# Rows of factors through DRAM instead of a selecting matmul, in one attention layer and one mixture of experts

## The chip, the cores and the metric

The kernel runs on one core of a Trainium2 chip. The time is that of the device, in microseconds (us), from the first to the last instruction of one launch. A core has five engines that run side by side, each through its own list of instructions in a fixed order: TensorE (PE, matmuls; its weight loads are shown as PEld), VectorE (DVE), ScalarE (ACT), GpSimd (POOL) and SyncE (SP). SyncE computes nothing; it issues DMAs, which sixteen DMA engines carry out. SBUF is the on-chip memory of 128 partitions, PSUM the memory that matmuls write, DRAM the memory off the core.

## The reference, cut to what matters

The program is a stack of eight layers on x of 4 x 512 x 128 float32: four times an attention and a feed-forward part, each followed by a layer norm of input plus output. The change touches the last two. The attention (index 3, "third" when counted from 0) has 16 heads of 64 and learned relative positions up to 16; the feed-forward part after it is a mixture of 16 experts of width 64, of which each token uses 4, and a shared one of width 128.

```python
attn = softmax(sim)                        # 16 heads, 512 x 512 each
out = attn @ v + (attn at the offsets) @ rel_v_table
out = out.reshape(B, T, 1024) @ Wo.T + bo
...
weights = top-4 of sigmoid(x @ w_gate.T), divided by their sum + 1e-6
combine[t, e] = the weight of expert e for token t, else 0
g = silu(x @ w1_e[e].T);  u = x @ w3_e[e].T
routed[t] = sum over e of combine[t, e] * (g * u) @ w2_e[e].T
```

Two factors matter here. Softmax's division is done late: the kernel adds up exp in passing and multiplies the attention's output by 1/sum, one factor for each head and query. And combine is one factor for each expert and token.

## The kernel before

Tokens stand in four blocks b of 512 (T). At build time a planner lays out each engine's list: an instruction's priority is its place in the program, and it may be passed by others as long as the planner believes its inputs not to be ready. On the chip that order is fixed; an engine whose next instruction waits does nothing else. The Python code is made of generators: `k.step(gs)` advances each of them by one `yield`, so the number of steps between two parts of the code sets how far apart they stand in priority. `k.bank("b")` takes one of two PSUM banks that all side work shares; `k.turn` makes side work take turns for them.

**The attention, class A3.** One unit t is one pair of heads of one block: 8 pairs, 4 blocks, 32 units. A unit has 8 items: four query blocks qc of 128, two heads e. `prep` computes the pair's Q and K with three matmuls each, splits them into a high and a low part (H by ScalarE at L1307, L by VectorE at L1308) and puts them into place with twelve copies from SBUF to SBUF (L1312), ten on SyncE's queue and two on GpSimd's. It also has SyncE store relative-position scores into DRAM (L1294) and read them back shifted (W, L1297). `score` makes two matmuls into one PSUM bank (L1344, L1345), adds W (L1347), takes the extreme of each row (L1349) and has ScalarE write p = exp (L1350), with the row's sum into `den`. The tile p holds both heads of a query block and has three buffers. `turn` runs two items later: four transposes (L219), a copy to PT (L1363), and, after the second head, a store of p's diagonal band to DRAM by SyncE (L1372, tile a3dpw). After the last item the band of the whole unit is read back along the diagonals (L1376), for which SyncE waits until the stores have landed. `tail` multiplies PT by V (L1393), adds the relative part (L1406, L1407) and copies the result to OT: 128 partitions are two heads of 64, the free axis is 512 queries.

Since one factor must reach the 64 partitions of its head, `fin` works on half a block, four pairs: 1/sum (L1422), its split into two parts (L1423, L1424), four transposes into 16 rows, a copy to lT (L1430), and for each pair a matmul of lT with a table of ones, `sel` (L1436), that puts each head's row, high plus low, on 64 partitions of a PSUM bank. VectorE multiplies OT by that bank (L1437). Then 16 matmuls project OT (L1447); after the second half a layer norm ends the block. `fin` runs at units 5, 9, 13, ..., 29 and once more at the end; from the same units on `half` projects the next half's values, through the same banks.

**The experts, class F3.** One step i is two experts (or the shared one) of a block, 9 steps to a block. `hidden` makes six matmuls, silu and a product (L2279), into h: 128 partitions are two experts of 64. `weigh`, four steps later, selects the two experts' rows with a matmul of `cT` with ones (L2287) and multiplies h by them (L2288). `out` adds h times w2 into the block's result (L2297). `gate` computes the weights: scores, two rankings (with a product by GpSimd at L1924), the weights (L2253), their split (L2256, L2257), transposes, and the copy to cT (L2265). It is started `ahead` = 7 steps before its block and advances `steps` = 2 times each step.

The two tables of ones are loaded by GpSimd's queue, which also clears the tiles for the rows (`rows16`).

## Time and profile before

| | us |
|---|---|
| three runs | 2252.24, 2237.65, 2249.25 |
| median | 2249.25 |
| the profiled execution, whole time | 2239.62 |
| its span in the profile | 2237.9 |
| units 9 to 12 of the attention (1700.6 to 1770.8) | 70.2 |
| of these TensorE / VectorE / ScalarE busy | 65.1 / 56.5 / 50.8 |
| last hidden products to the end (2216.9 to 2238.0) | 21.1 |

The granted TensorE clock was 0.965 of full speed over the span. The profile comes from one execution; all times in it count from the span's start. A "group" row gives an instruction's line in the kernel, its engine, operation, written and read tiles, count, busy time and the mean of one; by shapes it gives the least, median and longest time of one. The timeline gives start, length, engine and line; SPq means that SyncE was issuing a DMA, not that the DMA was running. The chain follows the execution back from its last instruction, at each step to what released it. Matmuls are pipelined: a matmul that follows another shows up with its full length in a group, but with the distance to the next one in the chain.

### The profile page before, as it was taken

The numbers are of one execution on the slowest core, as the hardware profiler recorded it, in microseconds if no ns is written. First come the engines' busy times: TensorE is split into PE (matmuls) and PEld (weight loads), VectorE is DVE, ScalarE is ACT, GpSimd is POOL, SyncE is SP. The second block draws the span as 40 slices with busy tenths as digits, with TensorE's granted clock in tenths as the row PEclk, the third lists the DMA queues.
The fourth block names the chain that finished last, engine by engine and source line by source line (L and its number), as shares of the span: only waits on it lengthen the run. The fifth ranks groups of instructions, "written<-read, shape, count | busy, mean of one in ns | idle before, by whom it ended". The sixth has DMA issues, their size and how long they took to land.

```text
span 2237.9 us, 43122 instructions
## 1 busy us (share of the span) xinstructions
PE 2025.4 (91%) x14400; PEld 1477.7 (66%) x14400; DVE 1664.1 (74%) x5592; ACT 1333.5 (60%) x2983; POOL 501.9 (22%) x706
## 2 busy tenths in 40 slices
PE   7999788888888999999999999998999999999897
PEld 4666566676665667676887665786666566666676
DVE  5778689888878677873777785544777877778787
ACT  3566787787734656665333666333777777767632
POOL 3222212111212532433000322531111111111220
PEclk9999999999978999999999999999999999999999
DMA  5321322021433454421021420604888878888400
GB/s 171 106 77 35 109 50 57 6 48 27 116 113 108 130 175 125 127 65 57 15 67 48 116 78 15 219 17 112 214 209 198 211 192 193 199 194 211 99 5 15
DMA packets 264918, 242.10 MB, mean 108 GB/s; under 512 B 106352, under 2 KB 190618, under 8 KB 263866
## 3 DMA queue, kind: packets, MB, share of 16 engines
q1 hardware_dynamic: 259146, 221.33, 37.2%
q0 software_dynamic: 5232, 17.50, 3.3%
q8 instruction: 115, 1.88, 0.3%
q14 instruction: 105, 0.86, 0.1%
q10 hardware_dynamic: 320, 0.52, 0.1%
HBM read 103.82 MB, written 74.32 MB: 80 GB/s over the span
## 4 chain that ended last, share of the span: by engine, by line
PE 59%; DVE 17%; ACT 10%; DMA 7%; issue 4%; POOL 2%; SPq 1%; ACTq 0%; POOLq 0%; DVEq 0%
PE t L219 5%; PE s L2129 4%; PE o L1393 3%; PE o L744 3%; PE s L695 3%; PE t L728 3%; PE o L1032 3%; PE b L313 3%; PE b L219 3%; PE o L2025 3%; DMA a3dpw<-p 2%; PE s L313 2%; PE b L315 2%; PE b L314 2%; PE s L315 2%
## 5 line engine op out<-in xcount | busy, mean ns | idle before, releaser
L985 DVE CUSTOM_DVE_ANT_0 junk<-w,a1mask 128x640 bf16<-128x640 f32 x256 | 203.1, 818 | 67.3 <-PE w L983 65.4
L219 PE MATMUL t<-ident,p 128*128 128x128 f32 x1280 | 201.9, 279 | 23.8 <-ACT p L1350 15.7
L772 ACT ACTIVATE Pt<-t 128x384 f32<-128x384 f32 (+1 forms) x384 | 179.5, 528 | 65.8 <-PE t L728 54.4
L219 PEld LDWEIGHTS t<-ident,p 128*128 128x128 f32 x1280 | 151.7, 142 | 81.0 <-ACT p L1350 39.0
L1363 ACT COPY PT<-t 128x512 f32<-128x512 f32 x256 | 149.9, 596 | 71.9 <-PE t L219 70.9
L1059 ACT ACTIVATE Pt<-t 128x512 f32<-128x512 f32 x256 | 149.1, 597 | 72.7 <-PE t L1058 44.5
L1350 ACT ACTIVATE p<-s,nb 128x512 f32<-128x512 f32 x256 | 178.6, 702 | 12.8 <-DVE nb L1349 8.4
L1349 DVE TENSOR_REDUCE nb<-s 128x1 f32<-128x512 f32 x256 | 175.0, 687 | 2.6
L1368 DVE CUSTOM_DVE_ANT_0 jk<-p,a3right 128x496 bf16<-128x496 f32 (+3 forms) x256 | 125.0, 488 | 29.2 <-ACT p L1350 17.8
L697 DVE CUSTOM_DVE_ANT_0 junk<-s,a0mask 128x128 bf16<-128x128 f32 (+3 forms) x256 | 114.2, 485 | 43.4 <-PE s L695 42.4
L697 DVE CUSTOM_DVE_ANT_0 junk<-s,a2mask 128x128 bf16<-128x128 f32 (+3 forms) x256 | 114.9, 484 | 28.3 <-PE s L695 27.9
L781 POOL TENSOR_SCALAR_AFFINE_SELECT Pt<-Pt 128x512 f32<-128x512 f32 x112 | 69.9, 636 | 249.0 <-ACT Pt L772 248.9
L1344 PE MATMUL s<-a3KT,a3QT 128*128 128x512 f32 x256 | 118.9, 465 | 7.3 <-DMA a3K<-L 4.1
L1347 DVE TENSOR_TENSOR s<-s,W 128x160 f32<-128x160 f32 (+1 forms) x256 | 81.1, 318 | 56.1 <-PE s L1345 55.2
L1393 PE MATMUL o<-PT,V 128*64 128x512 f32 x512 | 116.9, 599 | 0.5 <-ACT PT L1363 0.5
L1707 ACT ACTIVATE p<-sm,nb 128x128 f32<-128x128 f32 x256 | 100.6, 396 | 24.8 <-DVE nb L1705 24.3
L1345 PE MATMUL s<-a3K,a3Q 128*128 128x512 f32 x256 | 102.7, 401 | 0.1
L1705 DVE CUSTOM_DVE_ANT_0 sm<-s,band,rn 128x128 f32<-128x128 f32 x256 | 78.3, 344 | 26.5 <-PE s L1692 19.3
L1056 PE MATMUL t<-a1Q,a1K 128*128 128x512 f32 (+3 forms) x256 | 92.4, 366 | 6.2 <-ACT Pt L1059 3.6
L695 PE MATMUL s<-a0K,a0Q 128*128 128x256 f32 (+2 forms) x256 | 83.6, 387 | 14.0 <-DVE mx L697 6.8
L982 PE MATMUL w<-a1K,a1Q 128*128 128x256 f32 (+2 forms) x192 | 83.8, 437 | 9.3 <-DVE mx L985 8.3
L2012 ACT ACTIVATE sl<-s 128x512 f32<-128x512 f32 x64 | 38.0, 598 | 91.0 <-PE s L315 85.6
(494 smaller groups left out, 5812.7 us busy)
## 6 DMA issues: line engine op xcount, KB each, us to landing
W<-a3dsk SPq DMA_DIRECT2D x32, 640.0 KB
a1Q<-a1iq SPq DMA_DIRECT2D x32, 512.0 KB
a3dpw<-p SPq DMA_DIRECT2D x64, 160.0 KB
a3dpw<-p SPq DMA_DIRECT2D x64, 144.0 KB
a1K<-a1ik SPq DMA_DIRECT2D x64, 128.0 KB
a3Q<-a3dim SPq DMA_DIRECT2D x32, 256.0 KB
a3KT<-H POOLq DMA_DIRECT2D x64, 128.0 KB, 4.4
a3KT<-H SPq DMA_DIRECT2D x64, 128.0 KB
```

The source lines that it names most:

```text
L219: return self.nc.tensor.matmul(out.bitcast(x.dtype), x, i[:n, :n], is_transpose=True, start=start, stop=stop)
L695: self.scored = nc.tensor.matmul(s[:, :nm], self.qof(0, t, i)[:, qc * P:(qc + 1) * P], Ks[:, i, :nm], start=True, stop=True).ins
L697: nc.vector.tensor_tensor_reduce(junk[:, :n], s[:, :n], k.mask[:, 512 - n:512], 1.0, NEG, ALU.add, ALU.max, mx[:, qc, i:i + 1])
L772: ready = nc.scalar.activation(Pt[:, i, z:], s[:, z:], AF.Exp, scale=sc).ins
L985: nc.vector.tensor_tensor_reduce(junk, s.rearrange("p a n -> p (a n)")[:, T - n:T + m], k.mask[:, T - n:T + m], 1.0, NEG, ALU.add, ALU.max ...
L1059: nc.scalar.activation(Pt[:, i, :T], s, AF.Exp, scale=sc)
L1344: nc.tensor.matmul(s, QT[:, e, qs], KT[:, e, :], start=True, stop=False)
L1349: nc.vector.tensor_reduce(nb, s, AX.X, ALU.min)
L1350: nc.scalar.activation(p[:, e, :], s, AF.Exp, bias=nb, scale=-1.0, accum_out=den[:, qc, 2 * un + e:2 * un + e + 1])
L1363: self.copied[t] = nc.scalar.copy(PT[e][:, :, qc * P:qc * P + P], tb.rearrange("p (c n) -> p c n", n=P)).ins
L1368: nc.vector.tensor_tensor_reduce(jk[:, :nn], p[:, e, x0:], w["right"][:, :nn], 1.0, 0.0, ALU.mult, ALU.add, at[:, e, qc, 31:32])
L1393: m = nc.tensor.matmul(o[64 * e:64 * e + 64, :], V[:, kc, h * 64:h * 64 + 64], PT[e][:, kc, :], start=(kc == 0), stop=False)
```

## The change

The table of ones goes from the attention, and from blocks 1 to 3 of the experts; block 0 keeps its selecting matmuls. In their place a new helper, `spread_rows`, writes the rows of factors to DRAM with one DMA and reads each row back to 64 partitions with further DMAs, all on SyncE's queue; VectorE then multiplies by a tile in SBUF.

In the attention a new generator, `sums`, computes 1/sum and does the spreading at units 4, 8, ..., 32, six steps of the loop before `fin` uses it: one store of 8 rows of 2 KB and eight reads, each to 64 partitions of 2 KB. The rows are no longer split in two parts. Of the four result tiles two are new and two reuse buffers that are otherwise idle then.

In the experts the copy of the weights goes to DRAM in one DMA of 16 rows and comes back as two tiles of four pairs each, by four reads (64 partitions, four rows of 2 KB). The gate starts nine steps ahead instead of seven.

```diff
@@ -307,6 +307,17 @@
                 nc.gpsimd.tensor_tensor(l[:, s:e], w[:, :e - s], h[:, s:e].bitcast(F32), ALU.subtract)
                 yield
         return h, l, fill()
+
+    def spread_rows(self, dsts, rows, name):
+
+        nc = self.nc
+        d = self.dr.tile([rows.shape[0], T], F32, tag=f"rows{rows.shape[0]}", name=name, bufs=2)
+        nc.sync.dma_start(d, rows)
+        n = rows.shape[0] // 2 // len(dsts)
+        for i, dst in enumerate(dsts):
+            for e in range(2):
+                ap = [[0, 64], [2 * T, n], [1, T]] if n > 1 else [[0, 64], [1, T]]
+                nc.sync.dma_start(dst[64 * e:64 * e + 64], bass.AP(tensor=d.tensor, offset=d.offset + (2 * n * i + e) * T, ap=ap))
 
     def mm3(self, out, wh, wl, xh, xl):
         nc = self.nc
@@ -1121,7 +1132,6 @@
     c["c_step"] = st.reshape(64, 2, T)
     r = np.arange(16)[None, :]
     c["c_d16"] = (r < 16 - ql % 16).astype(np.float32)
-    c["c_sel3"] = heads(8)
     return c
 
 
@@ -1223,9 +1233,6 @@
         k, nc, d, pool, w = self.k, self.nc, self.k.d, self.pool, self.w
         w["right"] = pool.tile([P, 512], BF16, name="a3right")
         nc.gpsimd.dma_start(w["right"], d["c_right"])
-        w["sel"] = self.more.tile([P, 4, P], F32R, name="a3sel")
-        self.lT = k.rows16(self.more, "a3lT")
-        nc.gpsimd.dma_start(w["sel"], d["c_sel3"])
 
         self.QT, self.KT, self.Q2, self.K2 = ([pool.tile([P, 2, T], F32R, name=f"a3{n}{i}") for i in range(2)] for n in ("QT", "KT", "Q2", "K2"))
         for i in range(2):
@@ -1411,30 +1418,35 @@
         self.left -= 1
         yield
 
+    def sums(self, b, hf):
+
+        k, nc = self.k, self.nc
+        u = k.next()
+        rd = self.more.tile([P, 4, 8], F32, tag="rd", name=f"rd{u}", bufs=2)
+        nc.vector.reciprocal(rd, self.S[b][2][:, :, 8 * hf:8 * hf + 8])
+        yield
+        if b == NB - 1 and hf:
+            yield from k.turn()
+        ps = k.bank("b")
+        for c in range(4):
+            k.tr(ps[:8, c * P:(c + 1) * P], rd[:, c, :])
+        yield
+        lr = self.more.tile([P, T], F32, tag="rb", name=f"lrow{u}", bufs=2)[:8]
+        nc.scalar.copy(lr, ps[:8, :])
+        yield
+        rb = self.S["R", b, hf] = [pool.tile([P, T], F32, tag=tag, name=f"rb{u}{i}", bufs=n) for i, (pool, tag, n) in
+                                   enumerate(((self.early, "a3z", 1), (self.more, "rb", 2), (k.sh, "oT", 1), (self.more, "rb", 2)))]
+        k.spread_rows(rb, lr, f"a3rows{u}")
+        yield
+
     def fin(self, b, hf, X):
 
         k, nc, w, pool = self.k, self.nc, self.w, self.pool
         u = k.next()
-        den = self.S[b][2]
         wait = k.turn if b == NB - 1 and hf else lambda: ()
-        lr = self.more.tile([P, 4, 16], F32R, tag="lr", name=f"lr{u}", bufs=1)
-        rd = self.more.tile([P, 4, 8], F32, tag="rd", name=f"rd{u}", bufs=2)
-        nc.vector.reciprocal(rd, den[:, :, 8 * hf:8 * hf + 8])
-        nc.vector.tensor_copy(lr[:, :, 0:8], rd)
-        nc.vector.tensor_tensor(lr[:, :, 8:16], rd, lr[:, :, 0:8].bitcast(F32), ALU.subtract)
-        yield from wait()
-        ps = k.bank("b")
-        for c in range(4):
-            k.tr(ps[:16, c * P:(c + 1) * P], lr[:, c, :])
-        lT = self.lT
-        nc.scalar.copy(lT[:16], ps[:16, :])
-        yield
         for pr in range(4):
-            yield from wait()
-            ps = k.bank("b")
             OT = self.S["O", b, 4 * hf + pr]
-            nc.tensor.matmul(ps, w["sel"][:, pr, :], lT, start=True, stop=True)
-            nc.vector.tensor_tensor(OT, OT, ps, ALU.mult)
+            nc.vector.tensor_tensor(OT, OT, self.S["R", b, hf][pr], ALU.mult)
             yield
         if hf == 0:
             self.r = k.sh.tile([P, 4, P], F32, tag="r", name=f"r{u}", bufs=1)
@@ -1467,6 +1479,8 @@
                 gs.insert(0, self.prep(t + 1))
             if 1 <= t <= n:
                 gs.append(self.tail(t - 1))
+            if t >= 4 and t % 4 == 0:
+                sums = self.sums(*divmod((t - 4) // 4, 2))
             if t >= 5 and t % 4 == 1:
                 b, hf = divmod((t - 5) // 4, 2)
                 gs.append(self.fin(b, hf, Xs[b]))
@@ -1474,6 +1488,8 @@
                 gs.append(self.half(*divmod((t + 3) // 4, 2), Xs[(t + 3) // 8]))
             for j in range(8):
                 next(main, None)
+                if j == (self.la if t < n else 0) and t >= 4 and t % 4 == 0:
+                    gs.append(sums)
                 k.step(gs)
                 if t > n // 2:
                     k.tick()
@@ -2181,7 +2197,7 @@
 
 
     nm, span, keep = "f3", None, True
-    lag, ahead, steps = 4, 7, 2
+    lag, ahead, steps = 4, 9, 2
     banks = dict(s=4, t=1, o=1, b=2)
 
     def __init__(self, k):
@@ -2251,6 +2267,20 @@
         nc.vector.tensor_scalar(den, den, 1e-6, None, ALU.add)
         nc.vector.reciprocal(den, den)
         nc.vector.tensor_tensor(cw, cw, den[:, :, None].to_broadcast([P, 4, 16]), ALU.mult)
+        if b:
+
+            yield
+            yield from k.turn()
+            ps = k.bank()
+            for c in range(4):
+                k.tr(ps[:16, c * P:(c + 1) * P], cw[:, c, :])
+            yield
+            cr = pool.tile([16, T], F32, tag="cr", name=f"cr{u}", bufs=2)
+            nc.scalar.copy(cr, ps[:16, :])
+            cb = [pool.tile([P, 4, T], F32, tag="cb", name=f"cb{u}{i}", bufs=3) for i in range(2)]
+            k.spread_rows(cb, cr, f"f3rows{b}")
+            self.cT[b] = cb
+            return
 
         c2 = pool.tile([P, 4, 32], F32R, tag="c2", name=f"c2{u}", bufs=2)
         nc.vector.tensor_copy(c2[:, :, 0:16], cw)
@@ -2261,9 +2291,8 @@
         for c in range(4):
             k.tr(ps[:32, c * P:(c + 1) * P], c2[:, c, :])
         yield
-        cT = self.cTs[b % 2]
-        nc.scalar.copy(cT[:32], ps[:32, :])
-        self.cT[b] = cT
+        nc.scalar.copy(self.cT0[:32], ps[:32, :])
+        self.cT[b] = self.cT0
 
     def hidden(self, b, j):
         k, nc, w, pool = self.k, self.nc, self.w, self.pool
@@ -2283,6 +2312,9 @@
         k, nc, w = self.k, self.nc, self.w
         while b not in self.cT:
             k.step(self.gs)
+        if b:
+            nc.vector.tensor_tensor(h, h, self.cT[b][j // 4][:, j % 4, :], ALU.mult)
+            return
         cb = k.bank("t")
         nc.tensor.matmul(cb, w["sel"][:, j, :], self.cT[b], start=True, stop=True)
         nc.vector.tensor_tensor(h, h, cb, ALU.mult)
@@ -2310,7 +2342,7 @@
         self.w["2"] = k.load(pool, d["f3_w2"], [P, 9, P], "f3w2")
         self.w["sel"] = pool.tile([P, 8, P], F32R, name="f3sel")
         nc.gpsimd.dma_start(self.w["sel"], d["c_sel"])
-        self.cTs = [k.rows16(pool, f"f3cT{i}") for i in range(2)]
+        self.cT0 = k.rows16(pool, "f3cT0")
         gs = self.gs = [self.gate(0, Xs[0])]
         for x in "hl":
             self.w[f"1{x}"] = pool.tile([P, 2304], F32R, name=f"f3w{x}")
```

## The prediction

> **What bounds the kernel now.** I read the page's engine shares and its slices first, then the stages, then SyncE's line in time, then the chain.
>
> ```profile
> PE 2025.4 (91%) x14400; PEld 1477.7 (66%) x14400; DVE 1664.1 (74%) x5592; ACT 1333.5 (60%) x2983; POOL 501.9 (22%) x706
> DMA  5321322021433454421021420604888878888400
> ```
>
> TensorE is busy nearly everywhere, but the DMA slices say where the change lands: in the third attention (slices 28 to 38) the DMA engines are 80% busy and more, in the last experts nearly idle. By stages, units 9 and 10 of the attention (1700.6 to 1741 us) last 19.6 and 20.8 us with a DMA share of 0.84 and 0.92, units 11 and 12 last 15.2 and 14.6 us. (A unit is one pair of heads of one block; every fourth unit starts the projections of the next half and a `fin`.)
>
> SyncE's line between units 8 and 10, from the timeline (start, length, line, tile):
>
> ```profile
> 1692.22 0.36 SPq L1376 DMA_DIRECT2D at<-a3dpw  x1
> ...
> 1697.80 1.18 SPq L1312 DMA_DIRECT2D a3K<-L  x2
> 1699.08 1.61 SPq L1372 DMA_DIRECT2D a3dpw<-p  x3
> 1700.74 0.49 SPq L1294 DMA_DIRECT2D a3dsk<-bd  x1
> 1701.32 0.66 SPq L1298 DMA_DIRECT2D a3Q<-a3dim  x1
> 1704.64 0.36 SPq L1372 DMA_DIRECT2D a3dpw<-p  x1
> 1705.10 0.41 SPq L1297 DMA_DIRECT2D W<-a3dsk  x1
> 1709.06 0.36 SPq L1376 DMA_DIRECT2D at<-a3dpw  x1
> ```
>
> This is a loop through one queue. The store of a unit's last p (1704.64) must land before its band is read back (L1376, 1709.06, 4.1 us after the store's issue ended); behind that wait stand the ten copies of the next unit's operands (L1312, 1692.63 to 1698.98 in the round shown, 0.64 us apart); behind those stand the first three stores of p (1699.08). p has three buffers, so the exponentials of a unit's fourth query block wait for the first of these stores:
>
> ```profile
> 1703.16 0.70 ACT L1350 ACTIVATE p<-s,nb 128x512 f32<-128x512 f32 x1
> ...
> 1719.75 0.69 ACT L1350 ACTIVATE p<-s,nb 128x512 f32<-128x512 f32 x1
> ```
>
> They start 3.5 and 3.3 us after the issue of that store; in other units the same gap is as short as 2.2 us. So SyncE's line has some 1.2 us of room there, and TensorE's work has little more, as the chain shows around `fin`:
>
> ```profile
> 1710.05 0.43 PE b L1436
> ...
> 1711.38 0.38 PE b L1436
> ...
> 1713.25 0.24 PE b L1436
> ...
> 1714.51 0.25 PE b L1436
> ...
> 1719.75 1.46 ACT p L1350 x4
> 1721.22 4.19 DMA a3dpw<-p
> ```
>
> The selecting matmuls (L1436) lie on the chain, and so does the store that SyncE issues. Both limits stand side by side.
>
> **The change, part by part. Third attention, TensorE.** 32 selecting matmuls go. On the chain one `fin` pays 0.43 + 0.38 + 0.24 + 0.25 = 1.3 us for its four, so 8 x 1.3 = 10.4 us where TensorE sets the end; at the spacing of piped ones (0.23) it is 7.4, at their mean length (463 ns) 14.8. The transposes of 1/sum stay four to a `fin`.
>
> **VectorE.** The cast and the subtraction that split 1/sum go: 0.174 + 0.183 us, eight times, 2.9 us, beside VectorE's idle time (from 1555.5 to 2107 us it is busy 429 of 551 us): nothing. The products change operands:
>
> ```profile
> L1437 DVE TENSOR_TENSOR OT<-OT,b x32: 664/680/689, 1638.6 to 2115.1; 128x512 f32<-128x512 f32 x32
> L2152 DVE TENSOR_TENSOR r<-r,X x4: 682/692/693, 1459.4 to 1545.1; 128x512 f32<-128x512 f32 x4
> ```
>
> L2152 has the same shape with both operands in SBUF, 692 ns against 680 ns with one in PSUM. 56 products (32 and 24) times +0.012 is +0.7 us spread over an engine with room: nothing. What does go is the wait of a product for its selecting matmul (6.4 us in all, 9 times), which is inside the 1.3 us above or idle time.
>
> [...]
>
> **SyncE.** Each of the eight `sums` adds nine DMAs: one store of 8 rows and eight spreads to 64 partitions. The nearest row is L1312 (64 partitions of 2 KB, 0.60 us, 0.64 apart): 8 x 0.64 + 0.4 = 5.5 us. They are issued at step 5 of units 4, 8, ... 28 and at the end; by program order they stand behind the ten copies of unit 9 and ahead of the last stores of unit 8. SyncE idles from 1702.0 to 1704.64, 2.6 us; so the store at 1704.64 is 2.9 us late. In addition the spreads must wait until their own store has landed. The nearest rows are the loads at L1376: 3.0 us behind their store (issue ended 1689.23, load 1692.22) to 4.1 us. If SyncE has the other stores to issue meanwhile, that costs nothing; if it stands in the line alone, all 4.1. I take 1 us, because dsk, Q and two stores (about 2 us) can stand between, which is most of 2.9. So 4 us late, ends 3 and 7.
>
> Who waits: the load of the band (L1376), then unit 10's ten copies, then unit 9's first three stores, then the exponentials of p(9, qc3). Unit 10's copies had landed by 1717.3 and are first read at 1720.2: room 2.9 us, at the other units of that kind 1.6 to 5.4; so they come too late by about 1 us at worst. The exponentials have 1.2 us: 4 - 1.2 = 2.8 us late, at seven of eight `sums` (behind the eighth there is no unit): +20 us if TensorE has nothing else in its line, against -1.3 us each if it has. A unit ends with the later of the two lines, but TensorE has the matmuls of `half` and of the output (L1447) in its line there. I take the middle, (2.8 - 1.3) / 2 = +0.7 us a round: seven rounds +5, the last `fin` -1.3: **+4 us**, ends -10 and +20; with 7 us late +40.
>
> The spread traffic is 1 MB a round, 512 packets of 2 KB. The rows of such packets take 84 ns when the engines are free and 145 ns here: 2.7 to 4.6 us of 16 engines. The round of 70 us leaves (1 - 0.89) x 70 = 8 us free: hidden, unless it falls into units 8 and 12, where the share is 0.88 to 0.96.
>
> [...]
>
> **Last experts.** 24 selecting matmuls go, 24 x 0.235 = 5.6 us of TensorE; the cast and subtraction, about 0.4 us for each of three blocks. But TensorE waits there for VectorE, and the gate is what ends late:
>
> ```profile
> L2265 ACT CAST f3cT<-b x4: 559/574/577, 2139.8 to 2216.3; 32x512 fp32r<-32x512 f32 x4
> ```
>
> ```profile
> 2218.20 0.50 PE t L2287
> 2218.70 0.89 PE o L2297 x8
> 2219.59 0.39 PE t L2287
> 2219.98 0.89 PE o L2297 x8
> ```
>
> The last block's weights are ready (2216.3) when all its hidden products are done, and the tail is eight rounds of 1.28 us. Without the selecting matmul a round is 0.94 us: -2.7. `ahead` 9 starts the gate two steps earlier; a block's nine steps take 25.7 us, so 5.7 us earlier. The detour costs: store landed 3.0 after the copy, two issues 1.3 (L1298, the nearest of several rows to a partition, 0.66), landing 3.0, 1 MB at 84 ns a packet 2.7: 10.0 us; the second half comes 2.7 later, behind four rounds. So the first product moves by 10.0 - 5.7 = +4.3 us, the tail shrinks by 2.7, and of the 16 selecting matmuls ahead of it (3.8 us) I take two thirds, 2.6, since VectorE is the fuller engine there: **-1 us**, ends -6 and +6. SyncE has only the four output stores in this stage; behind a late product in VectorE's line stand the hidden products (L2279), and TensorE's banks behind those. GpSimd loses a table's load in each stage, and memsets of 0.54 us: off the path.
>
> **The sum.** +4 - 1 = +3 us on the profiled execution's 2239.62 us. That one is 9.6 us under the median of the three runs (2249.25), which themselves lie 14.6 apart; the four together have a mean of 2244.7. I forecast from there: **2247 us**, own range 2238 to 2258. About 1% (22 us) is what a measurement of this kernel can tell from no change.
>
> **Rivals.** *TensorE sets the end* (0.22): the planner puts the spreads into SyncE's idle time, all of the 10.4 us is gained and the experts give 6: 2244.7 - 16 = 2229. For it: the chain's L1436 pieces and the room of 3 to 5 us at unit 4k+2. Against it: the p stores behind the same queue. *SyncE's line sets it* (0.25): the spreads' wait for their store stands alone in the line, the queue behind it is 7 us late, and the exponentials wait 5.8 us in seven rounds: 7 x 5.8 = 41, minus what little TensorE keeps, 2280. It decides from the point at which the last store of a unit 4k is issued more than some 3 us later than now. For it: every wait for a landed store in this queue is real (61.0 us in 31 waits at L1376). Against it: SyncE idles 2.6 us right there. *The products wait in VectorE's line* (0.05): planned too early for rows that come late, 2 us in each of 8 `fin` and 3 blocks: +22, 2267. That the change doesn't do what it says has no room: the matmuls and their table are gone from the program. The forecast keeps 0.48.
>
> **Numbers.** 2228 to 2280 leaves out about 2 in 10. Faster by over 1% needs under 2227: 0.09. Slower by over 1%: most of the second rival and a tail of the forecast, 0.26. The rest is the same, 0.65.
>
> **What would show it.** Right: L1436 has gone and L2287 is down to 8; units 4k+1 last 19 to 21 us as before; the last p store of unit 4k is issued 3 to 5 us later against the unit's start; products still near 0.69 us; the experts end within 6 us of now. Wrong: units 4k+1 grow by over 4 us, with waits of L1350 for a3dpw (SyncE's line); or both heavy units shrink by over 1 us (TensorE). The sum is also wrong if the copies of unit 4k+1 themselves fall behind the spreads: they have no room at all (landed 1700.5, first read 1700.6).

## The result, and the profile after

| | before | after |
|---|---|---|
| median of the runs side by side, us | 2242.81 (six runs, 2237.65 to 2252.24) | 2276.04 (six runs, 2272.66 to 2281.11) |
| profiled execution, us | 2239.62 | 2278.61 |
| its span, us | 2237.9 | 2276.9 |
| granted TensorE clock over the span | 0.965 | 0.956 |

The ratio is 1.0144, 95% interval 1.0123 to 1.0165: the change costs 33 us. The forecast of no change was wrong; 2276 lies inside the stated range, close to the rival "SyncE's line sets it" (2280).

The page after, engine shares and the DMA slices:

```profile
PE 2032.4 (89%) x14344; PEld 1476.2 (65%) x14344; DVE 1666.6 (73%) x5570; ACT 1336.4 (59%) x2984; POOL 501.5 (22%) x703
DMA  5321411011434444312102322417888888898324
```

The 56 selecting matmuls have gone from the count (14400 to 14344), but TensorE is not busy for less: the span grew and its share fell by two points. New is the 3 2 4 at the end of the DMA slices, the rows of the last experts.

Where the 39 us between the two profiled executions lie, by the first and last score matmul (L1351) and the first block's weights (L2269 in after, cw) in the two traces:

| stage | before | after | |
|---|---|---|---|
| up to the first score of the attention | 1555.5 | 1559.5 | +4.0 |
| first to last score | 542.6 | 568.0 | +25.4 |
| last score to the first block's weights | 40.3 | 44.0 | +3.7 |
| from there to the end | 99.5 | 105.4 | +5.9 |

Nothing is changed in the first stage; it varied from 1553.5 to 1563.2 in all profiles of this study. The second is the loss. By units 4 to 30, four kinds of unit (t divided by 4 leaves 0, 1, 2, 3) have these mean lengths: before 14.99, 19.72, 20.16, 14.70; after 15.93, 24.78, 16.67, 15.50. A round of four went from 69.57 to 72.88, +3.3 us, and seven rounds make 23. Units 4k+1 grew by 5.1 and units 4k+2 gave 3.5 of it back; units 4k and 4k+3 grew by 0.9 and 0.8. Between the first and the last score TensorE was idle for 50.4 us instead of 31.4, and busy for 6.4 us longer (517.6 and 511.2) with 27 matmul records fewer, at a granted clock of 0.98 instead of 0.99. So about three quarters of the 25 us are idle time. The rest goes with slower matmuls; whether the clock fell because of the idle time, no run here separates.

The windows of units 9 and 10 in the kernel before (start:end, length, then busy time and count of PE, PEld, DVE, ACT, POOL, granted clock, DMA share, GB/s):

```profile
1700.60:1720.20 19.60, 18.43 (x109) 12.96 (x108) 15.31 (x43) 14.53 (x35) 2.17 (x4) 1.00 0.84 205
1720.20:1741.00 20.80, 19.18 (x107) 13.18 (x106) 18.02 (x59) 13.57 (x33) 3.47 (x5) 1.00 0.92 176
```

The same two units in the changed kernel:

```profile
1710.40:1735.90 25.50, 23.22 (x130) 16.57 (x129) 16.99 (x48) 15.50 (x37) 2.17 (x4) 0.93 0.87 209
1735.90:1752.20 16.30, 15.08 (x82) 9.45 (x80) 15.20 (x54) 12.15 (x29) 3.68 (x5) 1.00 0.79 177
```

Work moved from unit 10 into unit 9 (130 and 82 matmuls instead of 109 and 107): in the list that the planner laid out at build time, more of TensorE's other work now stands ahead of unit 10's first score. That is why one unit's length alone would mislead, and why the sum over the round is the number to read.

SyncE's line in the changed kernel over the place where the prediction had looked, units 8 and 9 (start, length, line, tile; unit 9 starts at 1710.40):

```profile
1708.04 1.19 SPq L1319 DMA_DIRECT2D a3K<-L  x2
1709.32 1.07 SPq L1379 DMA_DIRECT2D a3dpw<-p  x2
1710.49 0.34 SPq L315 DMA_DIRECT2D a3rows<-lrow  x1
1710.93 0.37 SPq L1379 DMA_DIRECT2D a3dpw<-p  x1
1711.36 1.31 SPq L1301 DMA_DIRECT2D a3dsk<-bd  x1
1712.76 0.54 SPq L1305 DMA_DIRECT2D a3Q<-a3dim  x1
1713.39 5.03 SPq L320 DMA_DIRECT2D rb<-a3rows  x8
1718.52 0.53 SPq L1379 DMA_DIRECT2D a3dpw<-p  x1
1719.81 0.36 SPq L1304 DMA_DIRECT2D W<-a3dsk  x1
1722.60 0.36 SPq L1383 DMA_DIRECT2D at<-a3dpw  x1
...
1729.47 1.63 SPq L1379 DMA_DIRECT2D a3dpw<-p  x3
```

The order is the predicted one: ten copies, two stores of p, the store of the rows, one store, two further DMAs, the eight reads (5.03 us), and only then unit 8's last store of p. There is next to no gap in front of the reads (0.09 us): their store had landed while SyncE issued three other DMAs. Behind them the band load and the ten copies for unit 10 follow, and unit 9's first three stores of p only at 1729.47. The first of them has been issued 19.6 us behind the unit's start, in the kernel before 15.9; in the mean of the units 4k+1 it is 20.0, before 14.6.

The last link of the predicted path, the exponentials of unit 4k+1's fourth query block, begin 24.3 us behind the unit's start in that mean, before 18.0. In five of the seven units they begin 1.9 to 4.5 us behind the first store's issue (before 2.5 to 4.1), in the other two some 8 us. ScalarE's idle time that ended with the landing of a store of p is 2.8 us in these units, once (before 0.3). So most of the lateness of the exponentials isn't a wait seen at run time. The lists were laid out anew with the new DMAs in them, and the runs don't tell an order planned around a late line from the late line itself.

### The profile page after: what moved, and what is told of

It reads as the page before. It is cut to its first block, busy times and chain, and to the rows that moved or that the text cites. A ratio compares the mean times of both kernels' runs of the same rounds, so it can differ in the third digit from the quotient of the medians.

```text
span 2276.9 us, 43133 instructions
## 1 busy us (share of the span) xinstructions
PE 2032.4 (89%) x14344; PEld 1476.2 (65%) x14344; DVE 1666.6 (73%) x5570; ACT 1336.4 (59%) x2984; POOL 501.5 (22%) x703
## 4 chain that ended last, share of the span: by engine, by line
PE 59%; DVE 15%; ACT 11%; DMA 8%; issue 4%; SPq 1%; POOL 1%; ACTq 0%; DVEq 0%; POOLq 0%
PE t L219 5%; PE s L2145 4%; PE s L706 3%; PE o L755 3%; PE t L739 3%; PE o L1400 3%; PE o L1043 3%; PE b L219 3%; PE o L2041 2%; PE b L324 2%; PE s L324 2%; PE s L326 2%; PE b L326 2%; PE s L325 2%; PE b L325 2%
## 5 line engine op out<-in xcount | busy, mean ns | idle before, releaser
L1354 DVE TENSOR_TENSOR s<-s,W 128x144 f32<-128x144 f32 (+1 forms) x256 | 81.2, 318 | 88.4 <-PE s L1352 87.7
L1351 PE MATMUL s<-a3KT,a3QT 128*128 128x512 f32 x256 | 121.3, 474 | 6.7 <-DMA a3K<-L 4.8
L1723 ACT ACTIVATE p<-sm,nb 128x128 f32<-128x128 f32 x256 | 100.6, 396 | 24.7 <-DVE nb L1721 24.3
```

Of the source, the lines that this page charges most:

```text
L1351: nc.tensor.matmul(s, QT[:, e, qs], KT[:, e, :], start=True, stop=False)
```

## The experiments

All ratios are to runs of the kernel before on the same chip; a ratio of 0.001 is 2.2 us. Besides the ratio, one reading from SyncE's line is given for most: how long after the start of a unit 4k its last store of p has been issued (mean over units 4, 8, ... 28), and when its band is loaded.

### The two parts alone

`att_only` is the changed attention with the experts of before, `exp_only` the reverse. Against the changed kernel, the core of each:

```diff
 att_only, class F3
-    lag, ahead, steps = 4, 9, 2
+    lag, ahead, steps = 4, 7, 2
...
-        if b:
-            nc.vector.tensor_tensor(h, h, self.cT[b][j // 4][:, j % 4, :], ALU.mult)
-            return
 exp_only, class A3
-            nc.vector.tensor_tensor(OT, OT, self.S["R", b, hf][pr], ALU.mult)
+            nc.tensor.matmul(ps, w["sel"][:, pr, :], lT, start=True, stop=True)
+            nc.vector.tensor_tensor(OT, OT, ps, ALU.mult)
```

> The attention's part alone; the experts as before. Theory Q: SyncE's queue is the bound in units 4k and 4k+1. The spreads put the last store of unit 4k about 4 to 5 us later, the exponentials of unit 4k+1 follow, and each of seven rounds loses about 3 us: 20 to 28 us slower than before, most of the 33 us of the whole change. Rival E: the experts lose most, since their rows come late for the last block; then this kernel is within 10 us of before.

> The experts' part alone (with the gate nine steps ahead); the attention as before. Theory Q: 4 to 10 us slower, from the last block, whose rows land some 10 to 15 us after the copy of its weights while the gate comes at best 6 us earlier. Rival E: 20 us slower or more. If the tail's 2.7 us and the 5.6 us of TensorE were won as forecast: 1 to 6 us faster.

The attention alone: 2278.77 us, 1.0148 (1.0133 to 1.0163), the whole loss. The experts alone: 2255.18 us, 1.0042 (1.0027 to 1.0057), 9 us. The two don't add up: with both, the loss is that of the attention alone. So the experts' part costs by itself and nothing on top.

In `exp_only`'s profile the attention took 540.8 us from its first score to that of unit 31 (531.6 before), although every engine's instructions up to there stand in the same order. `before_again`, the kernel before once more, is the check on how far such a reading can be trusted:

> The kernel before once more, unchanged: how far the attention's stage differs from one execution to the next with the same order of instructions. Units 0 to 31 took 531.6 us in the first profile and 540.8 in the profile of the experts' part alone, where the attention's code and order are those of before. If executions differ, 530 to 542 us; if only the addresses in DRAM differ, within 3 us of 531.6.

It took 533.2 us, and two later kernels with the attention of before 531.6 and 537.0. So readings of one and the same order lie between 531.6 and 540.8 us, and one profile's reading of this stage is good to some 5 to 9 us; the shares below rest on ratios.

### Issues or bytes

`att_quarter` reads a quarter of the bytes with as many DMAs (three quarters of the factors are left out, and each product uses the quarter four times); `att_pool` leaves the bytes and lets GpSimd issue the reads; `att_poolq` does both. Against `att_only`:

```diff
 att_quarter
-   nc.sync.dma_start(dst[64 * e:64 * e + 64], ... ap=[[0, 64], [1, T]])
+   nc.sync.dma_start(dst[64 * e:64 * e + 64, 0:P], ... ap=[[0, 64], [1, P]])
 att_pool
-   nc.sync.dma_start(dst[64 * e:64 * e + 64], ...)
+   nc.gpsimd.dma_start(dst[64 * e:64 * e + 64], ...)
```

> The attention's part alone, with spreads of 128 of the 512 columns; the product uses these for all four query blocks, so three quarters of the factors are left out. Nine DMAs and SyncE's time stay, a quarter of the bytes goes. Theory Q: within 4 us of the attention's part alone. Rival B, the 1 MB of each round collides with the other transfers: at least two thirds of the loss goes, within 8 us of before.

> The attention's part alone, with the eight spreads issued by GpSimd instead of SyncE; the store of the rows stays with SyncE. The bytes stay, 5 us of SyncE's line in each round go. Theory Q: 10 to 25 us faster than the attention's part alone. Rival B: no faster than it, within 4 us. GpSimd's own line could spoil it: the band's split (POOL a) and two copies of each unit stand there too.

> The attention's part alone with both cures: the eight reads issued by GpSimd and only 128 of 512 columns read (three quarters of the factors are left out, the product repeats the first quarter). GpSimd's issues alone gave back 17 us of 33, the quarter of the bytes alone 11. If the two costs are separate and add up, 28 us come back and the time is 3 to 8 us over the kernel before, what is left being the last `fin`'s way through DRAM (+6 us from the last score to the experts' first weights). If both are one cost seen twice (the delay of the last p store), it is no better than GpSimd's issues alone: 13 to 18 us over the kernel before.

| | us | ratio | loss, us | last p store of units 4k | band load | first to last score, one profile | last score to the end, one profile |
|---|---|---|---|---|---|---|---|
| before | | | | 19.2 | 22.7 | 542.6 | 139.8 |
| att_only | 2278.77 | 1.0148 (1.0133 to 1.0163) | 33 | 24.1 | 28.4 | 563.7 | 151.8 |
| att_quarter | 2267.6 | 1.0091 (1.0062 to 1.0121) | 20 | 24.6 | 26.6 | 559.8 | 146.8 |
| att_pool | 2261.79 | 1.0072 (1.0043 to 1.0100) | 16 | 18.6 | 23.0 | 553.6 | 146.1 |
| att_poolq | 2249.41 | 1.0011 (0.9992 to 1.0030) | 2.5 | 18.4 | 21.8 | 544.0 | 142.2 |

Each cure alone leaves half, both together leave nothing that can be told from zero: two separate costs, some 13 us for the bytes and 17 for the issues (each good to about 7), which add up. Against expectation, a quarter of the bytes did not take away two thirds (the rival) nor leave all (the theory). The last column says where: by these profiles 4 to 6 us of each cost lie behind the last score, not in the rounds of four units.

What the bytes cost when SyncE's line is clear can be read in `att_pool`'s list of waits (engine, line, tile, what it waits for: total, times, longest):

```profile
DVE OT L1449 <- DMA rb<-a3rows: 19.9, 14, 6.1
```

and in that of `att_poolq`:

```profile
DVE OT L1450 <- DMA rb<-a3rows: 6.6, 7, 1.9
```

The products wait for their factors, 19.9 us in the one, 6.6 in the other: 13.3 less, about as much as the time. That agrees with the prediction's third rival, given 0.05, as what the bytes do here. In the changed kernel the same wait is 6.9 us in four, in `att_only` 4.9 in seven; that SyncE's late line hides it there is a guess.

And `att_poolq` says one thing more: with most of both costs gone, all 32 selecting matmuls of the attention are still away, and no time is gained. Its rounds take 69.18 us against 69.57 (69.20 to 70.52 in four more profiles with the attention of before). A quarter of the bytes and the store on SyncE are still there, so a gain of a few us may be hidden; no run took the matmuls away and nothing else.

### Issues as such, or their place

`before_nine` adds to the kernel before, at seven of the places, nine DMAs of next to no bytes that nobody reads:

```diff
+        d = k.dr.tile([8, 4], F32, tag="nine", name=f"nine{u}", bufs=2)
+        nc.sync.dma_start(d, X[:8, 0, 0:4])
+        for i in range(8):
+            nc.sync.dma_start(self.junk[64 * (i % 2):64 * (i % 2) + 64, i // 2, :], bass.AP(tensor=d.tensor, offset=d.offset + 4 * i, ap=[[0, 64], [1, 4]]))
```

> The kernel before, with its selecting matmuls, and at seven of the eight places of `sums` nine further DMAs on SyncE's queue that nobody reads: one store of 8 rows of 16 bytes, eight reads of 16 bytes to 64 partitions. Almost no bytes (8 KB a round), and no work taken from any engine. Theory Q: SyncE's line alone makes units 4k+1 2 to 4 us longer, 12 to 28 us over the kernel before, the last p store of units 4k 3 to 5 us later. Rival B or the planner's other order: within 6 us of the kernel before.

2252.44 us, 1.0015 (1.0001 to 1.0030): 3 us, where 12 to 28 were expected. SyncE spends as long on them; its line around unit 9's start (1703.1) in `before_nine`:

```profile
1700.26 1.07 SPq L1372 DMA_DIRECT2D a3dpw<-p  x2
1701.39 5.56 SPq L1424 DMA_DIRECT2D a3junk<-nine  x8
1707.05 1.08 SPq L1372 DMA_DIRECT2D a3dpw<-p  x2
...
1710.00 0.36 SPq L1376 DMA_DIRECT2D at<-a3dpw  x1
```

5.56 us for the eight, as in the changed kernel. But their data had long been there, so in six of the seven rounds the planner put them, or in two of these the six or four that it hadn't put earlier still, behind the second store of p. Here they fill the gap that SyncE has before the last p is ready, the third and the last store go out together at 1707.05, and the band is loaded 20.7 us behind the unit's start. In the mean of the units 4k the last store is at 20.8 and the band load at 22.8, as before (22.7); units 4k+1 take 21.39 us, 1.7 longer, and units 4k+2 0.9 less. Nine issues cost next to nothing there. In the changed kernel the rows are copied late (ScalarE, 1707.8), and the reads take up the gap and more.

In the seventh round, unit 28 (start 2040.4), the planner gave the empty DMAs the very place that they have in the changed kernel:

```profile
2054.93 1.07 SPq L1372 DMA_DIRECT2D a3dpw<-p  x2
2056.06 0.38 SPq L1422 DMA_DIRECT2D nine<-X  x1
2056.54 0.36 SPq L1372 DMA_DIRECT2D a3dpw<-p  x1
...
2058.22 5.03 SPq L1424 DMA_DIRECT2D a3junk<-nine  x8
2063.35 0.53 SPq L1372 DMA_DIRECT2D a3dpw<-p  x1
```

The last p store of unit 28 is issued 23.5 us behind its start, as in the changed kernel (23.7), and units 28 to 30 take 51.9 us: 48.3 to 49.1 in five profiles with the attention of before, 52.2 in the changed kernel. The other six rounds, units 4 to 27, take 422.9, in those five 420.8 to 430.1. So by this profile all of the run's 3 us lie in the one round with the changed kernel's order, and seven such rounds would make some 20, near the 17 put down to the issues. It is a single round, and `att_poolq` took 51.6 us for the same units with its last store at 18.6, so something else can lengthen them, too.

These runs also speak against the path that the prediction took from the line to the unit's end. In `before_nine` the first p store of units 4k+1 is issued 18.8 us behind the unit's start and the exponentials of the fourth block begin at 23.6, nearly as late as in the changed kernel (20.0 and 24.3), and six of its seven rounds lose nothing by it.

`att_late` moves the real ones to the next unit, and `att_latepool` has GpSimd issue them there:

```diff
         nc.scalar.copy(lr, ps[:8, :])
-        yield
+        for _ in range(8):
+            yield
 fin
+        for _ in range(5):
+            yield
         for pr in range(4):
```

> The attention's part alone with the store and the eight reads of each `sums` moved later by seven steps, into unit 4k+1 (all eight reads stand between its third and its last p store on SyncE's line), and the products of `fin` five steps later. Same DMAs, same bytes, same engine. In the kernel before, the copies for the unit behind a unit 4k are issued 1.3 to 1.6 us ahead of its start, those for the unit behind a unit 4k+1 4.4 to 8.1 us ahead. Theory Q, place (what costs is where in SyncE's line the nine issues stand): the last p store of units 4k is back at 18 to 20 us behind the unit's start, and 10 to 20 of the 33 us come back, 13 to 23 us over the kernel before. Rival B (the bytes, wherever they stand) or W (the work of nine issues, wherever they stand): within 5 us of the attention's part alone, 28 to 36 us over the kernel before.

> The same, with the eight reads issued by GpSimd. With the reads in their old place GpSimd's issues left a loss of 16 us, of which a quarter of the bytes left 2.5: 13 us were put down to the bytes. If those 13 us are bytes in the wrong place (landing while the last p stores and the band of unit 4k go through the same 16 DMA engines), the later place takes back most of them: 2 to 9 us over the kernel before. If they are bytes as such: 12 to 18 us over.

`att_late`: 2261.97 us, 1.0066 (1.0033 to 1.0099), a loss of 15 (7 to 22) instead of 33, with the same DMAs, bytes and engine. The last p store of units 4k is back at 20.6, the band load at 23.3. SyncE's line in it (unit 9 starts at 1702.4, unit 10 at 1719.8):

```profile
1706.68 0.36 SPq L1379 DMA_DIRECT2D a3dpw<-p  x1
...
1709.84 0.36 SPq L1383 DMA_DIRECT2D at<-a3dpw  x1
...
1720.04 5.92 SPq L320 DMA_DIRECT2D rb<-a3rows  x8
1726.06 0.53 SPq L1379 DMA_DIRECT2D a3dpw<-p  x1
```

Unit 8's last store is undisturbed; now unit 9's is late (issued 24.2 behind its start, 21.0 before), but more room lies behind that one, as the expectation had it. In three of the seven rounds the reads come only behind that last store. The total is in the range of theory Q, but the stages say something else: from the first to the last score `att_late` took 558.2 us (`att_only` 563.7, before 542.6), from there to the end 140.4 (151.8 and 139.8). By this one profile, its fastest execution, two thirds of what the two stages gave back lie behind the last score, where only the eighth `sums` stands. So this run doesn't show that the place within the rounds is what counts.

`att_latepool`: 2257.62 us, 1.0054 (1.0034 to 1.0073), a loss of 12 (8 to 16), on the border between the two answers of its expectation. It can't be told from `att_late` nor from `att_pool` (16): what SyncE's issues cost at this place is less than the runs resolve, some 8 us, and that the later place saves any of the bytes' 13 us isn't shown. How the bytes act there isn't shown either: the products wait 9.5 us in `att_latepool`, but in `att_late`'s list of waits there is none.

### A second way to fewer issues

`att_four` reads two rows at once, to 128 partitions:

```diff
-   for e in range(2):
-       nc.sync.dma_start(dst[64 * e:64 * e + 64], ... ap=[[0, 64], [1, T]])
+   nc.sync.dma_start(dst, ... ap=[[T, 2], [0, 64], [1, T]])
```

> The attention's part alone, but each `sums` reads its four tiles back with four DMAs of 128 partitions instead of eight of 64: the same 1 MB a round, five DMAs in SyncE's line instead of nine. Theory Q (issues in SyncE's line): about half of what the move of the eight reads to GpSimd gave back (17 us) returns, so 7 to 12 us faster than the attention's part alone, some 22 to 26 us over the kernel before. Rival B (the bytes in the rings): the same bytes, within 4 us of the attention's part alone (+33 us). A third answer: a DMA of 128 partitions takes SyncE twice as long to issue (over 1.2 us each); then it is within 4 us, too, and the issue times in the trace say so.

2405.41 us, 1.0704 (1.0673 to 1.0735): 157 us slower, which no theory expected. Its timeline of SyncE and its windows around unit 9 (1725.4 to 1764.2):

```profile
1726.39 11.04 SPq L318 DMA_DIRECT2D rb<-a3rows  x4
1737.48 7.22 SPq L1377 DMA_DIRECT2D a3dpw<-p  x1
```

```profile
1725.00:1735.00 10.00, 8.82 (x48) 4.98 (x46) 6.53 (x19) 7.63 (x19) 1.04 (x2) 1.00 0.54 121
1735.00:1745.00 10.00, 3.23 (x22) 2.53 (x20) 1.85 (x4) 1.45 (x3) 0.00 (x0) 0.83 0.13 50
```

The first two are issued in 0.56 and 0.52 us, no longer than a read of 64 partitions (median 0.59 in the changed kernel), but at the third SyncE is held up, and the DMA share is 0.13, about two engines of sixteen: 37 packets of 84 ns in each 1.5 us. This pattern moves here at the rate of two DMA engines (37 x 84 ns / 1.5 us = 2.1). At that rate one read takes 128 x 84 ns / 2 = 5.4 us, four follow each other, and the store behind them in the line holds SyncE for another 7.22 us. So this run tells nothing of half as many issues, only that in this form four reads don't do for the eight; the last p store of units 4k is at 35.4 and units 4k+1 take 41.3 us, but the products wait as well, 140.6 us in 32, and the two can't be told apart.

### Is the loop through the stores the bound of the kernel before?

The prediction took SyncE's loop for one of two limits that stand side by side. `before_actst` lets ScalarE issue the stores of p, `att_actst` does the same in `att_only`.

```diff
-            nc.sync.dma_start(dpw.rearrange("(h c) p n -> p h c n", h=2)...
+            nc.scalar.dma_start(dpw.rearrange("(h c) p n -> p h c n", h=2)...
```

> The kernel before with the stores of p issued by ScalarE instead of SyncE (four of 0.4 us a unit). Theory Q says that units 4k+3 and 4k are bound by the loop of SyncE's queue: ten copies, then the stores of p, then the exponentials that need p's three buffers. With the stores on another queue the loop is cut: units of 14.7 us go to 13.5 or less, 10 to 30 us faster than before. Rival T: TensorE bounds these units, and the change is worth nothing or costs ScalarE's 1.6 us a unit: 0 to 20 us slower.

> The attention's part with the same edit: the stores of p issued by ScalarE. Theory Q: the spreads then delay only the read of the band and the next copies, which have room in unit 4k+2; the loss against the kernel before with the same edit falls from 33 to under 12 us. If the spreads hurt by their bytes or through the products, the loss stays over 20 us.

`before_actst` took 2267.72 us, 1.0096 (1.0077 to 1.0115): not faster but 22 us slower. Taking the stores out of the loop did not uncover a faster kernel; units 4k+3 grew from 14.70 to 16.79, and TensorE's first score matmuls waited 9.0 us for the copy into a3KT (2.3 before) and 6.0 for the stores. Why is open: the stores' new place on ScalarE is itself a change of the line. `att_actst` took 2271.71 us, 1.0113 (1.0085 to 1.0140). Between these two kernels the rows cost 4 us instead of 33 (good to about 7). That agrees with the theory, as far as it goes: where the stores of p don't stand behind the reads, most of the loss is away. But both kernels have a new limit that may hide it.

### The experts

`ahead9` is the kernel before with `ahead` = 9 alone; `exp_12` is the kernel before with rows through DRAM for blocks 1 and 2 only.

```diff
 ahead9
-    lag, ahead, steps = 4, 7, 2
+    lag, ahead, steps = 4, 9, 2
 exp_12, against exp_only
-        if b:
+        if b in (1, 2):
```

> The kernel before with the gate nine steps ahead instead of seven, nothing else. If starting two gates side by side is what delays the first block (first weights at 2147 us instead of 2138 in the profile of the experts' part alone), this is 3 to 8 us slower than before; if it is the detour, within 2 us.

> The kernel before with the experts' part for blocks 1 and 2 alone (the last block and the first keep the selecting matmul; `ahead` is 9, which alone changed nothing). In the experts' part alone, the body from the first gate's weights to the last one's was 3.7 us shorter and the tail behind it 9.3 us longer. If that split holds, this keeps the first and not the second: 2 to 5 us faster than the kernel before. If the gain of the body was only the planner's trade for the tail: within 2 us. The attention in it has the kernel before's order; if its units 0 to 31 take 540 us again instead of 532, the experts' part changes the attention by something that the instruction order doesn't show.

`ahead9`: 2244.1 us, 0.9998 (0.9983 to 1.0014). Two steps more bring nothing. `exp_12`: 2252.5 us, 1.0018 (1.0003 to 1.0033), 4 us slower where 2 to 5 faster were hoped for. From the first hidden product to the end its profile shows 121.9 us, `exp_only`'s 124.2, the kernel before 119.0 and 117.3 (twice), `ahead9` 119.1. The gates do come earlier (91.4 us behind the first hidden product for the last one, before 95.4), but the hidden products end 6.6 us later (105.2 behind the first, before 98.6): the 3.7 us shorter body was the planner's trade for the tail, not a gain.

The tail of `exp_only`, from the chain (start, length, what):

```profile
2221.60 0.59 ACT cr L2274
2222.20 3.62 DMA f3rows<-cr
2225.84 0.58 SPq L320
2226.47 7.05 DMA cb<-f3rows
2233.61 0.70 DVE h L2311
2234.36 9.05 PE o L2324 x64
```

and of the changed kernel:

```profile
2248.60 0.58 ACT cr L2279
2249.20 1.57 DMA f3rows<-cr
2250.78 0.58 SPq L320
2251.41 0.61 SPq L320
2252.12 0.57 SPq L320
2252.74 10.67 DMA cb<-f3rows
2263.44 0.70 DVE h L2316
2264.18 3.85 PE o L2329 x32
```

In the one the first half of the factors is what ends late, in the other the second: the fifth product at 2263.44 waits for the last read, 10.67 us on its way. The two tiles are 1024 packets of 2 KB; their median in this stretch is 166 ns, 1024 x 166 ns / 16 = 10.6 us.

## Why the prediction was wrong

**Third attention, SyncE: the line right, what it costs wrong.** "4 us late, ends 3 and 7" measured 4.7 (last p store 19.2 to 23.9), the reads 5.0 to 5.7 us (8 x 0.64 = 5.1 predicted), and the wait for the store cost less than the 1 us set for it (0.09 us in front of the reads in each of the seven rounds). The step that failed is the next: "I take the middle, (2.8 - 1.3) / 2 = +0.7 a round". A round grew by 3.3 us, from both costs together: with a quarter of the bytes (`att_quarter`) by 2.2, with the reads on GpSimd (`att_pool`) by 1.1. So SyncE's issues are worth nearer to that pair's upper end, 2.8, than to its middle, and TensorE's -1.3 doesn't show: `att_poolq` has rounds of 69.18 against 69.57 with the matmuls gone and most of the delays, too. Of two limits that were said to stand side by side, the delay of one cost most of its length here, and the relief of the other gave nothing that the runs resolve. The 10.4 us that the first part put down for TensorE "if TensorE sets the end" were the matmuls' share of the chain, not what their removal is worth.

The links behind the line are not confirmed. The band load, the first stores of unit 4k+1 and its last exponentials all came later, as predicted, but the waits that should carry the delay are hardly there (2.8 us), and in `before_nine` stores and exponentials nearly as late cost nothing in six rounds. How a late line becomes a longer round stays open.

The rival that named this (SyncE's line) had the right queue but the price too high: 5.8 us a round by a line 7 us late; the line is 4.7 late, its own condition ("more than some 3 us later than now") is met, and the price of a round is 3.3, of which bytes are a part. That its total came within 4 us of the result is partly luck, by the following terms.

**The spread bytes: "hidden" failed.** They cost 13 us (`att_quarter` against `att_only`, `att_poolq` against `att_pool`). The reasoning was a share of a round: 8 us of engine time free in 70, 2.7 to 4.6 wanted. But the reads land in units with a DMA share of 0.81 to 0.94 in the changed kernel (0.89 to 1.00 in the 12 us behind the first read's issue), ahead of a product that needs them or of a band load behind them. The mean over a round says nothing of that. That it is these landings that cost the time is argued; the products' waits in `att_pool` speak for it.

**The last `fin`: -1.3 was measured as +3.7** from the last score to the first gate's weights in the changed kernel, and from +2.4 to +7.1 in `att_only`, `att_quarter`, `att_pool` and `att_poolq`. The nearest reason, that no unit follows to cover the way through DRAM, doesn't hold: in `att_late` and `att_latepool` the last rows go the same way (reads 6.9 and 7.4 us behind the last score, 6.8 in the changed kernel; last product 22.4 and 20.4 behind it, 19.2 there), and this stage changed by +0.3 and -0.8. The windows of the first 24 us behind the last score, in the kernel before:

```profile
2098.00:2122.00 24.00, 19.91 (x119) 13.57 (x118) 17.42 (x63) 12.38 (x24) 11.42 (x27) 1.00 0.23 66
```

and in `att_only`:

```profile
2123.00:2147.00 24.00, 17.97 (x77) 10.92 (x76) 15.32 (x38) 10.45 (x22) 10.99 (x23) 0.79 0.41 111
```

TensorE does 77 matmuls instead of 119, and at a granted clock of 0.79. What keeps it from the others is open.

**VectorE held.** The products, L1449 and L2316, have medians of 682 and 681 ns:

```profile
L1449 DVE TENSOR_TENSOR OT<-OT,rb x32: 679/682/973, 1644.5 to 2146.7; 128x512 f32<-128x512 f32 x32
L2316 DVE TENSOR_TENSOR h<-h,cb x24: 677/681/691, 2214.7 to 2265.2; 128x512 f32<-128x512 f32 x24
```

Both operands now lie in SBUF, and nothing is gained over the 680 ns with one in PSUM (L1437 before).

**The last experts: -1 was measured as +9 alone (`exp_only`).** The +5.9 between the profiles of before and after, from the first gate's weights to the end, isn't this part's: `att_only`, with the experts of before, has +5 there. The 10.0 us of detour was exact for the first product (copy at 2248.6, product at 2258.7: 10.1), but three terms were mis-sized. The bytes went by 84 ns a packet, which `att_four` shows at a DMA share of 0.13; with 2 MB at once the median is 166, and the second half came 4.7 us behind the first instead of 2.7. "`ahead` 9 starts the gate two steps earlier, 5.7 us earlier" gave nothing (`ahead9`). And what the gates gained on the hidden products, these ended later (`exp_12`). One reading of the code was wrong, too: GpSimd doesn't lose a table's load in the experts, since block 0 keeps its table; it is off the path. Why this part's 9 us vanish beside the changed attention isn't settled: `att_only` has the experts of before, and they took it 131.5 us from the first hidden product, the changed kernel 130.8.

**What remains open**: what bounds the kernel before in the third attention. Moving the stores of p uncovered no gain (`before_actst`, which has a cost of its own), and the removal of the selecting matmuls none that shows (`att_poolq`). No version here beats the kernel before.

## What to carry to other kernels

Where a chain runs through a queue and an engine in turns, price an added transfer by its place in the queue: nine issues a round cost 3 us in all where six of seven rounds had them in front of the queue's gap, and some 17 where every round had them ahead of the last store. Look for what stands behind the new work, up to the buffer that comes free last, and reckon with most of the delay as the cost (here a round 3.3 us longer with a store 4.7 us late, the bytes' part in it); don't set against it what another engine saves until a run has shown that the saving comes through. And price bytes by the DMA share of the very units in which they land (here 0.81 to 0.94), at the length of a packet under that load (here a median of 144 ns in the third attention and 166 in the last experts).

## What the runs showed of the hardware

- A read with the pattern 2 x 64 (repeated) x 512 elements, from DRAM to 128 partitions, moved at a DMA share of 0.13, about two of sixteen engines (`att_four`: 36 to 37 packets of 2 KB, 84 ns each, started in each 1.5 us). Where the changed kernel's eight reads of 64 x 512 to 64 partitions landed in unit 9, 193 packets of 2 KB started in 1.5 us (1719.4 to 1720.9), all transfers counted: at 84 ns or more each, the work of at least ten engines. The DMA share was 1.00 over the 12 us from 1713.4 on.
- Packets of 2 KB that read the same rows took 84 ns at a DMA share of 0.13 (`att_four`) and a median of 166 ns where 1024 of them started within 10.7 us (the changed kernel's last experts); the last of the four reads, 2 MB in all, landed 10.7 us behind its issue.
- SyncE took as long for a read of 64 x 16 bytes (median 0.59 us, `before_nine`) as for one of 64 x 2 KB (0.59, the changed kernel): issuing doesn't go by bytes here. GpSimd took 0.53 us for each of the same reads (`att_pool`).
- In some windows the granted clock was lower where TensorE did less: behind the last score, in windows of 24 us, 1.00 with 119 matmuls (before), 0.86 with 105 (changed kernel), 0.79 with 77 (`att_only`); 0.83 with 22 matmuls in the ten microseconds in which `att_four`'s line was blocked, 1.00 with 48 in the ten before. It doesn't hold everywhere: in the changed kernel unit 9 had 0.93 with 130 in 25.5 us, and from 2151 to 2171 the clock was 1.00 with 86 in 20 us. Which of the two follows from the other isn't shown.
